# Softmax denominators turned and compacted on VectorE before the check and the reciprocal, with the steps of a two-layer graph kernel in a new order

## The chip, the cores and the metric

The kernel runs on one core of one Trainium2 chip. The metric is the device time of one launch in microseconds (us); lower is better. Engine names as in the profile: PE is TensorE (PEld its weight loads), DVE is VectorE, ACT is ScalarE, POOL is GpSimd, SP is SyncE, which issues the DMAs.

## The reference

128 graphs of 128 nodes with 256 features (float32) and an integer adjacency pass through two layers. Layer 0 is masked multi-head attention with a feed-forward block; layer 1 is two graph-attention (GAT) steps with a feed-forward block.

```python
# layer 0 (8 heads of 32, four relations; the random adjacency holds only 0 and 1)
q, k = src @ Wq + bq, src @ Wk + bk
attn = softmax(q k^T / sqrt(32), axis=-1)
out  = sum over r of (attn * (adj == r)) @ (src @ Wv[r] + bv[r])
x    = LN(src + out @ Wo + bo)
x    = LN(x + gelu(x @ W1 + b1) @ W2 + b2)
# layer 1
h = gat(gat(x, adj, W1, a1), adj, W2, a2)     # leaky_relu scores, softmax over axis 1
h = LN(x + h)
x = LN(h + relu(h @ w_ff1 + b_ff1) @ w_ff2 + b_ff2)
```

## The kernel before

`fast_pass` assumes that adj is 0 or 1 and that no softmax leaves a safe range without its maximum subtracted. It records extremes on the way (`c_adj`, `c_gat`, `c_att`), and the step `checks` compares them at the end. Only if one fails does `general_pass` compute everything again. In the profiled execution `fast_pass` alone does the work.

The 128 graphs go in 32 groups of 4 (`G`), so a group is 512 tokens. A group passes through steps written as Python generators: each `yield` ends one piece of a step, and a string of tokens says which piece of which step of which group comes next. `FRONT` covers the start, `STEADY` is used once for each middle group (29 times), `TAIL` ends. In a token `f:1*2`, `f` is the step, 1 the group relative to the current one, 2 the number of pieces. The steps: `q` projections, `a` attention, `n0`..`n3` layer norms, `t0`..`t2` the transposed copies of x, `f` the first feed-forward block, `l` the GAT layer, `k` the second feed-forward block, `in`, `rest` and `out` the loads and stores. The recording is under `manual_schedule`, so each engine executes its instructions in exactly the recorded order, and so does SP with its DMA issues. An engine that waits in its order holds all that stands behind it.

The feed-forward blocks and projections use Strassen-like products (7 in place of 8) into the PSUM banks `fa`, `fe` and `seeded`; DVE and ACT combine the parts. `seeded` is drained by ACT (`p16`) or DVE before PE adds the next product to it. A matmul instruction of float32 shows as two matmuls in the trace.

Attention does two graphs at a time, as "pair 0" and "pair 1". For one pair: `scores` (PE, tile `ps`), exp (ACT, tile `e`), `masked` (DVE, `pm` = e times adj), then `sums`. In `sums` the PE writes the unnormalised output into `pav`, and the denominators into `pden`, by a matmul with a block of ones of 32 columns. So each denominator, of one head and one query, stands 32 times below each other: rows 0 to 31 of `pden` are one head, and all 32 are equal. `pden` holds 128 x 512 numbers, of which 128 x 16 differ. ACT copies it into `rd` with a running sum for the check (L810) and runs over it a second time for the lower bound (L813); DVE takes the reciprocal of all 128 x 512 numbers, in two halves (L817, L819), and multiplies `pav` by it into `oT` (L822). `pden` of pair 0 lies in the bank `fe`, that of pair 1 in one of the two banks `s`; `pav` has one bank, `av`, for both pairs. From `oT` comes the output projection (`pwo`).

Of the kernel before, what the change touches and what calls it, by code (L numbers as in the profile page):

```python
# [99 lines left out]


FRONT = """
bo:0 q:0*4 a:0*3 q:0*2 a:0*5 q:0*2 a:0*3 output_bias q:1 a:0*2 n0:0 q:1*2 n0:0*2 q:1 a:1*2 n0:0*2
b1 a:1 q:1 w1 q:1 t0:0*3 bo:1 a:1 in:2 q:1 f:0*2 a:1*2 f:0*2 a:1*2 gelu a:1 q:1 f:0*3 wqk f:0 a:1
f:0 w2 f:0*4 gw f:0 a:1*2 gw f:0*3 gw f:0 a:1*2 f:0 n0:1 q:2 n0:1*4 f:0*2 q:2 f:0 gw q:2 t0:1*2
n1:0 q:2*2 t0:1 q:2 f:1 n1:0*3 u2 n1:0 q:2*2 f:1*3 q:2 t1:0*2 c1 q:2 f:1*3 l:0 f:1*2 u1 q:2 l:0*3
q:2 l:0*2 f:1 q:2*2 l:0 f:1 q:2 f:1 l:0 f:1 wv l:0 f:1 l:0*2 exp f:1 a:2 l:0*3 f:1 q:2 a:2 q:2*2
l:0 q:2 f:1*2 q:2*2 n2:0 q:2 n2:0 q:2 a:2 n2:0 f:1 q:2 n2:0 q:2 f:1 q:2*2 n2:0 f:1 q:2*2 t2:0*2
in:3 a:2*2 f:1 t2:0 n1:1 k:0 a:2 k:0*2 a:2 n1:1*4 a:2 k:0*3 t1:1*2 k:0 a:2 k:0*2 a:2 k:0 l:1 a:2
bo:2 k:0*3 l:1 k:0*2 a:2 k:0 l:1 a:2 k:0*2 a:2 l:1 n0:2 k:0 n0:2*3 q:3 l:1 k:0*2 n0:2  # L110
"""
STEADY = """
l:0 t0:1 q:2 t0:1*2 q:2 f:1 q:2*2 f:1 q:2 l:0 k:-1 f:1 q:2*2 f:1*2 n3:-1 f:1 l:0 gelu q:2*2 f:1
l:0 n3:-1 f:1 l:0 n3:-1 q:2*3 f:1*5 q:2*2 f:1 l:0*2 f:1 l:0 out:-1 f:1 a:2 l:0 rest:2 f:1 q:2
a:2*2 q:2*3 l:0 q:2*2 n2:0 q:2*2 n2:0*3 f:1*2 q:2*2 n2:0 f:1 q:2*2 f:1 exp t2:0 in:3 q:2*2 t2:0
f:1 n1:1 a:2*2 t2:0 k:0*3 a:2 n1:1 k:0 a:2 n1:1*3 a:2 k:0*2 a:2 k:0*3 t1:1 a:2 k:0 bo:2 t1:1 a:2
l:1 k:0*2 a:2 l:1 k:0 l:1 a:2*2 n0:2 k:0 n0:2 k:0 l:1 n0:2 k:0 n0:2 k:0 l:1 k:0*4 q:3 n0:2
"""
TAIL = """
k:-1 t0:1*3 f:1 l:0 f:1*2 l:0 f:1*3 n3:-1 l:0 gelu f:1*3 l:0 f:1 n3:-1*2 l:0*2 f:1*3 l:0*2 f:1  # L120
exp l:0 f:1*2 l:0 n2:0 f:1*2 n2:0*4 t2:0 f:1 out:-1 t2:0 f:1*3 n1:1 t2:0 k:0 n1:1 k:0*2 n1:1 k:0
n1:1*2 k:0*2 t1:1 k:0 t1:1 l:1 k:0 l:1*4 k:0 l:1 k:0*2 l:1 k:0*2 l:1*4 k:0 l:1*2 k:0 l:1 k:0 l:1
n2:1 k:0 n2:1*4 k:0*3 t2:1*2 k:0*2 t2:1 k:1*3 n3:0*2 k:1*4 n3:0 k:1 out:0 k:1*7 checks k:1*5
z:1*2 k:1*2 z:1
"""


# [8 lines left out]
def fast_pass(ctx, tc, a, out):  # L136
# [5 lines left out]
    nc = tc.nc  # L142
# [268 lines left out]

    def turned(S, i):
        n = f"{i}_{S['g']}"
        yT = w2p.tile([P, NCH, T], F32, tag="yT", name="yT_" + n)
        for p in range(G // 2):
            pT = S["pT", i, p].rearrange("p (h b c) t -> p h b c t", h=2, b=2)
            for c in range(NCH):
                o = yT[:, c, p * D : (p + 1) * D].bitcast(U16)
                nc.scalar.copy(  # L419
                    o.rearrange("p (b t h) -> p h b t", b=2, h=2), pT[:, :, :, c, :]  # L420
                )
            if p == 0:
                yield
        S["xT", i + 1] = yT
        yield
        if i == 1:
            return

        S["yS", i + 1] = ys = w1p.tile([P, 4, TH], F32, tag="yS", name="yS_" + n)
        a11, a21, a12, a22 = (yT[:, c, h * TH : (h + 1) * TH] for c in range(2) for h in range(2))  # L430
        nc.vector.tensor_sub(ys[:, 2], a11, a21)
        nc.vector.tensor_add(ys[:, 0], a21, a22)
        nc.vector.tensor_sub(ys[:, 1], a22, ys[:, 2])
        nc.vector.tensor_sub(ys[:, 3], a12, ys[:, 1])
        yield

    def ffn(S, i, wa, ba, func, wb_):

        n = f"{i}_{S['g']}"
        yT, ys, x = S["xT", i], S["yS", i], S["x"]  # L440
        a11, _, a12, a22 = (yT[:, c, h * TH : (h + 1) * TH] for c in range(2) for h in range(2))
        s1, s2, s3, s4 = (ys[:, m] for m in range(4))
        hT = w1p.tile([P, NF, T], F32, tag="hT", name="hT_" + n)
        h2 = w1p.tile([P, NF // 2, TH], F32, tag="h2", name="h2_" + n)
        h3 = w1p.tile([P, NF // 2, TH], F32, tag="h3", name="h3_" + n)
# [45 lines left out]
        pa = begun(0)  # L491
        nc.scalar.copy(seeded, pa)
        yield
        for r in range(RN):
            rs = slice(2 * r, 2 * r + 2)
            pe = ps_1.tile([P, T], F32, tag="fe", name=f"ph7_{n}_{r}")
            product(pe, T3, s3, r, True)
            p7 = w1p.tile([P, T], F32, tag="p7", name=f"p7_{n}_{r}")
            nc.scalar.copy(p7, pe)
            yield  # L500
            product(seeded, T2, s2, r)
            p16 = w1p.tile([P, T], F32, tag="p16", name=f"p16_{n}_{r}")
            nc.scalar.copy(p16, seeded)  # L503
            yield
            product(pa, B21, a12, r)
            activated(pa, r, 0, 0)
            yield
            product(seeded, T1, s1, r)
            nc.vector.tensor_add(hidden(1, 1, r), halves(seeded), halves(p7))  # L509
            activated(None, r, 1, 1)  # L510
            yield
            product(pe, T4, a22, r)
            nc.vector.tensor_add(hidden(0, 1, r), halves(pe), halves(p16))  # L513
            activated(None, r, 0, 1)
            yield
            if r + 1 < RN:
                pa = begun(r + 1)
                yield
            product(seeded, B22, s4, r)
            activated(seeded, r, 1, 0)  # L520

            nc.vector.tensor_sub(h3[:, rs], hidden(0, 0, r), hidden(0, 1, r))
            nc.vector.tensor_add(hidden(0, 1, r), hidden(0, 1, r), hidden(1, 1, r))
            nc.vector.tensor_sub(h2[:, rs], hidden(1, 1, r), h3[:, rs])
            if r + 1 < RN:
                nc.scalar.copy(seeded, pa)
            yield
# [245 lines left out]
    def sums(S, p):  # L773


        assert {(1, 0, p), (1, 1, p)} <= S["have"]
        e, pm = S["e", p], S["pm", p]
        n = f"{S['g']}_{p}"

        pool, tag = (ps_1, "fe") if p == 0 else (ps_s, "s")  # L780
        pden = pool.tile([P, 2, NCH, P], F32, tag=tag, name="pden_" + n)
        pav = ps_1.tile([P, 2, NCH, P], F32, tag="av", name="pav_" + n)

        def plain():
            for s in range(HC):
                nc.tensor.matmul(
                    pden[s * DH : (s + 1) * DH], k.ones, e[:, s], start=True, stop=True
                )


        late = S["g"] > 1
        if not late:
            plain()
        for u in range(2):
            v = S["v"][:, 2 * p + u]
            for c in range(NCH):
                for r, m in enumerate((e, pm)):
                    for s in range(HC):
                        d0 = r * D + c * P + s * DH
                        nc.tensor.matmul(  # L800
                            pav[s * DH : (s + 1) * DH, u, c, :],
                            v[:, d0 : d0 + DH], m[:, s, u, c, :],
                            start=(r == 0), stop=(r == 1),
                        )
# [5 lines left out]
        nc.scalar.activation(  # L810
            rd, pden, AF.Identity, accum_out=c_att[:, 1, g, p : p + 1]
        )
        nc.scalar.activation(  # L813
            pden, pden, AF.Relu, bias=k.lo, scale=-1.0, accum_out=c_att[:, 0, g, p : p + 1]
        )
        yield
        nc.vector.reciprocal(rd[:, 0], rd[:, 0])  # L817
        yield
        nc.vector.reciprocal(rd[:, 1], rd[:, 1])  # L819
        for u in range(2):  # L820
            bs = slice((2 * p + u) * P, (2 * p + u + 1) * P)
            nc.vector.tensor_mul(oT[:, :, bs], pav[:, u], rd[:, u])  # L822
        yield
# [139 lines left out]
    def checks():  # L963

        gat = c_gat.rearrange("p g l b -> p (g l b)")
        for i, (t, op) in enumerate(
            (
                (gat, ALU.min), (gat, ALU.max), (c_att[:, 1].rearrange("p g u -> p (g u)"), ALU.max),
                (c_att[:, 0].rearrange("p g u -> p (g u)"), ALU.max), (c_adj, ALU.max),
            )  # L970
        ):
            nc.vector.tensor_reduce(ext[:, i : i + 1], t, AX.X, op)
        nc.vector.tensor_scalar(ok[:, 0:1], ext[:, 0:1], LO, None, op0=ALU.is_ge)
        nc.vector.tensor_scalar(ok[:, 1:3], ext[:, 1:3], HI, None, op0=ALU.is_le)
        nc.vector.tensor_scalar(ok[:, 3:5], ext[:, 3:5], 0.0, None, op0=ALU.is_le)

# [415 lines left out]
```

## Time and profile before

| | before |
|---|---|
| median of 3 runs | 2732.59 us (2731.11 to 2733.99) |
| profiled execution, device time | 2731.53 us |
| its span, first to last instruction | 2729.7 us |
| granted TensorE clock, mean | 0.994 |
| PE / DVE / ACT / POOL busy | 98% / 85% / 64% / 5% |
| reciprocals of the denominators on DVE (L817, L819) | 128 of about 1.74 us |
| passes over the denominators on ACT (L810, L813) | 128, 596 and 657 ns, each with a read of its sum of 0.2 us |

The profiled execution is 1.83 us longer than its span and 1.06 us shorter than the median. Busy shares are averages over the whole span. The marker ACT L581 (one element through gelu or exp, which loads that table) stands twice in a group, and every second one comes 82.7 us after the one before in the middle of the span: this is the time of one group. A matmul's end is modelled in the trace, and a matmul that follows another starts before that end, so the PE's pace is read from the distance of starts rather than from its durations.

### The profile page before, as it was taken

What the parts mean: (1) busy time and instruction counts of PE and PEld (TensorE: products, weight loads), DVE (VectorE), ACT (ScalarE), POOL (GpSimd) and SP (SyncE); (2) the same over time, 40 slices, a digit from 0 to 9 for tenths busy, and PEclk for the clock granted to TensorE, in tenths of its full rate; (3) what the DMA queues carried; (4) which work ended last, traced back from release to release, by engine and by line L of the source; (5) the groups of instructions that cost most, each with busy time, mean ns of one, the idle gap of its engine ahead of it and who ended that gap; (6) DMA issues with size and microseconds to landing.
All of it is one profiled execution on the core that took longest, in us unless ns stands there. A gap on an engine that the chain in (4) does not pass through costs nothing.

```text
span 2729.7 us, 53540 instructions
## 1 busy us (share of the span) xinstructions
PE 2664.3 (98%) x20917; PEld 2308.5 (85%) x20917; DVE 2322.0 (85%) x5612; ACT 1750.6 (64%) x3777; POOL 142.3 (5%) x137
## 2 busy tenths in 40 slices
PE   8999999999999999999999999999999999999997
PEld 5887888888888888888888888889888888888876
DVE  4878889888889888889888898888898888888876
ACT  3556676666676666666665766666766666666663
POOL 0000000000000000000000000000000000000000
PEclk8999999999999999999999999999999999999999
DMA  6012111212121221121222112121112111212210
GB/s 188 16 28 55 51 44 36 59 48 52 48 54 36 57 49 51 44 52 43 51 55 51 44 37 57 50 54 48 50 36 59 47 51 44 59 36 51 47 36 25
DMA packets 271899, 136.43 MB, mean 50 GB/s; under 512 B 210092, under 2 KB 250392, under 8 KB 271640
## 3 DMA queue, kind: packets, MB, share of 16 engines
q1 hardware_dynamic: 270536, 132.55, 20.6%
q8 instruction: 166, 2.72, 0.4%
q14 instruction: 93, 0.76, 0.1%
q10 hardware_dynamic: 1104, 0.40, 0.1%
HBM read 65.68 MB, written 16.90 MB: 30 GB/s over the span
## 4 chain that ended last, share of the span: by engine, by line
PE 53%; DVE 34%; ACT 8%; issue 3%; DMA 1%; SPq 1%; POOL 0%; ACTq 0%; DVEq 0%; POOLq 0%
PE ph L454 9%; PE seeded L454 9%; PE po L463 9%; DVE x L379 6%; PE seeded L463 6%; DVE pm L768 4%; PE pw L919 4%; PE pwo L835 4%; DVE st L350 3%; ACT hT L478 3%; PE pqqa L680 3%; PE pqqb L680 3%; PE pav L800 2%; PE py L932 2%; DVE rd L817 2%
## 5 line engine op out<-in xcount | busy, mean ns | idle before, releaser
L393 ACT COPY planes<-x 128x512 uint16<-128x512 uint16 x384 | 216.5, 629 | 216.6 <-DVE x L379 216.6
L419 ACT COPY yT<-pT 128x512 uint16<-128x512 uint16 x384 | 267.3, 769 | 94.1 <-DMA pT<-planes 93.2
L368 POOL TENSOR_TENSOR rs<-rs,mhalf 128x4 f32<-128x4 f32 x129 | 140.1, 1086 | 2535.9 <-DVE rs L367 2535.9
L454 PE MATMUL seeded<-yS,w_L_gnn_w_ff 128*128 128x256 f32 x768 | 210.2, 396 | 2.0 <-DVE hT L509 0.7
L509 DVE TENSOR_TENSOR hT<-seeded,p 128x512 f32<-128x512 f32 x128 | 88.1, 688 | 139.2 <-PE seeded L454 139.1
L454 PE MATMUL seeded<-yS,w_L_gnn_W 128*128 128x256 f32 x768 | 201.9, 385 | 0.3 <-ACT p L503 0.2
L454 PE MATMUL ph<-yT,w_L_gnn_W 128*128 128x256 f32 x768 | 197.7, 380 | 3.8 <-ACT yT L419 3.8
L350 DVE BATCH_NORM_STATS2 st<-x 128x6 f32<-128x256 f32 x512 | 192.2, 417 | 6.8
L454 PE MATMUL ph<-yT,w_L_gnn_w_ff 128*128 128x256 f32 x768 | 195.4, 383 | 0.8 <-ACT hT L478 0.8
L454 PEld LDWEIGHTS seeded<-yS,w_L_gnn_w_ff 128*128 128x128 f32 x768 | 135.3, 189 | 69.2 <-ACT yT L419 24.3
L463 PEld LDWEIGHTS po<-w_L_gnn_W,hT 128*128 128x128 f32 x1536 | 186.1, 192 | 4.7
L463 PE MATMUL po<-w_L_gnn_w_ff,hT 128*128 128x128 f32 x1536 | 187.1, 275 | 0.0
L463 PE MATMUL po<-w_L_gnn_W,hT 128*128 128x128 f32 x1536 | 187.0, 275 | 0.0
L463 PEld LDWEIGHTS po<-w_L_gnn_w_ff,hT 128*128 128x128 f32 x1536 | 181.7, 192 | 1.7
L454 PEld LDWEIGHTS seeded<-yS,w_L_gnn_W 128*128 128x128 f32 x768 | 142.1, 190 | 30.2 <-ACT p L503 9.2
L454 PEld LDWEIGHTS ph<-yT,w_L_gnn_W 128*128 128x128 f32 x768 | 146.2, 191 | 24.6 <-ACT yT L419 4.6
L454 PEld LDWEIGHTS ph<-yT,w_L_gnn_w_ff 128*128 128x128 f32 x768 | 141.0, 190 | 25.7 <-ACT hT L478 1.4
L768 DVE TENSOR_TENSOR pm<-e,adj 128x512 f32<-128x512 f32 x256 | 159.2, 683 | 0.2 <-ACT e L758 0.2
L478 ACT ACTIVATE hT<-hT,c_L_gnn_b_ff 128x256 f32<-128x256 f32 x256 | 113.1, 514 | 70.6 <-DVE hT L513 41.1
L800 PE MATMUL pav<-pm,v 128*32 128x128 f32 x2048 | 126.0, 275 | 25.1 <-DVE v L695 19.2
L758 ACT ACTIVATE e<-ps 128x512 f32<-128x512 f32 x256 | 135.4, 602 | 4.8 <-PE ps L750 4.8
L463 PE MATMUL seeded<-w_L_gnn_W,hT 128*128 128x128 f32 x1024 | 130.6, 279 | 1.0 <-DVE hT L561 1.0
(196 smaller groups left out, 6350.6 us busy)
## 6 DMA issues: line engine op xcount, KB each, us to landing
xT<-in_xT_dram SPq DMA_DIRECT2D x32, 512.0 KB, 3.9
x<-in_x_dram SPq DMA_DIRECT2D x32, 512.0 KB, 6.2
out_dram<-x SPq DMA_DIRECT2D x31, 512.0 KB, 3.1
spread<-hbm SPq DMA_DIRECT2D x59, 256.0 KB, 3.2
adj<-in_adjT_dram SPq DMA_DIRECT2D x32, 256.0 KB, 4.5
pT<-planes SPq DMA_TRANSPOSE x192, 3.1
w_L_gnn_W<-in_L_gnn_W_dram SPq DMA_DIRECT2D x8, 256.0 KB, 8.3
w_L_gnn_w_ff<-in_L_gnn_w_ff_dram SPq DMA_DIRECT2D x8, 256.0 KB, 5.0
```

The costliest lines, as they stand in the source:

```text
L350: nc.vector.bn_stats(st[:, b % 2, :], S["x"][:, b, :])
L368: nc.gpsimd.tensor_tensor(rs[:, bs], rs[:, bs], k.mhalf[:, bs], op=ALU.pow)
L379: nc.vector.scalar_tensor_tensor(x[:, b, :], x[:, b, :], mv[:, b, 0:1] if first else rs[:, b : b + 1], g if first else be, op0=ALU.subtrac ...
L393: nc.scalar.copy(planes[:, :, b], words)
L419: nc.scalar.copy(o.rearrange("p (b t h) -> p h b t", b=2, h=2), pT[:, :, :, c, :])
L454: nc.tensor.matmul(bank[:, s * TH : (s + 1) * TH], wa[:, form, 0, f * P : (f + 1) * P], m, start=start and s == 0, stop=True, skip_group_c ...
L463: nc.tensor.matmul(bank[:, s * P : (s + 1) * P], m[:, f, s * P : (s + 1) * P], wb_[:, form, f, :], start=start and s + f == 0, stop=True, ...
L478: nc.scalar.activation(o[:, s], o[:, s] if src is None else src[:, s * TH : (s + 1) * TH], func, bias=ba[:, f : f + 1],)
L680: nc.tensor.matmul(bank[:, s * TH : (s + 1) * TH], *ops, start=start and s == 0, stop=True, skip_group_check=True,)
L758: nc.scalar.activation(e[:, s], pss[s], AF.Exp, scale=SCALE)
L768: nc.vector.tensor_mul(pm[:, s], S["e", p][:, s], S["ad"][:, pair(p), None, :].to_broadcast([P, 2, NCH, P]),)
L800: nc.tensor.matmul(pav[s * DH : (s + 1) * DH, u, c, :], v[:, d0 : d0 + DH], m[:, s, u, c, :], start=(r == 0), stop=(r == 1),)
```

## The change

In `sums`, ACT's two passes are gone. DVE turns each 32 x 32 block of `pden` into `rd` (one instruction, 128 x 512); after the turn the distinct denominators stand in every 32nd column, 16 in a partition. DVE takes their minimum and their sum for the check, then the reciprocal of these 128 x 16, and a second turn, fed by a broadcast view of the 16 columns, spreads them over `rd` again. The bank of `pden` is now freed by DVE's first turn. `checks` compares a minimum with the lower bound where it compared a sum of excesses with 0. The pieces of `sums` are cut at other places: one `yield` ahead of the turn, one behind the second turn. In `turned` the tile is entered earlier, in `ffn` the yS views are taken later; neither adds an instruction. The three order strings are new throughout.

```diff
 STEADY = """
-l:0 t0:1 q:2 t0:1*2 q:2 f:1 q:2*2 f:1 q:2 l:0 k:-1 f:1 q:2*2 f:1*2 n3:-1 f:1 l:0 gelu q:2*2 f:1
-l:0 n3:-1 f:1 l:0 n3:-1 q:2*3 f:1*5 q:2*2 f:1 l:0*2 f:1 l:0 out:-1 f:1 a:2 l:0 rest:2 f:1 q:2
-a:2*2 q:2*3 l:0 q:2*2 n2:0 q:2*2 n2:0*3 f:1*2 q:2*2 n2:0 f:1 q:2*2 f:1 exp t2:0 in:3 q:2*2 t2:0
-f:1 n1:1 a:2*2 t2:0 k:0*3 a:2 n1:1 k:0 a:2 n1:1*3 a:2 k:0*2 a:2 k:0*3 t1:1 a:2 k:0 bo:2 t1:1 a:2
-l:1 k:0*2 a:2 l:1 k:0 l:1 a:2*2 n0:2 k:0 n0:2 k:0 l:1 n0:2 k:0 n0:2 k:0 l:1 k:0*4 q:3 n0:2
+f:0 a:1*2 k:-1 a:1 n1:0 t2:-1 a:1 in:2 n1:0 a:1 k:-1*2 a:1 k:-1 n1:0 k:-1*3 n1:0 a:1 n1:0 t1:0
+k:-1*2 a:1 bo:1 l:0 k:-1 a:1 k:-1 a:1 t1:0 k:-1*2 a:1 k:-1 l:0 k:-1 n0:1 l:0 k:-1 n0:1*4 k:-1 q:2
+k:-1 q:2 l:0 k:-1 t0:1 l:0 t0:1 q:2 k:-1*2 q:2 l:0 t0:1 f:1*4 l:0*2 q:2 k:-1 f:1 n3:-1 f:1*2 l:0
+f:1 q:2*2 l:0 f:1 n3:-1*2 f:1 q:2*2 gelu f:1*3 q:2*2 out:-1 f:1 q:2 l:0 q:2 l:0 q:2*2 l:0 f:1 a:2
+l:0 f:1 q:2 a:2 rest:2 q:2*2 a:2 q:2 l:0 n2:0 q:2 f:1 q:2*3 n2:0*2 f:1 q:2*2 n2:0 q:2 f:1 q:2*3
+n2:0 t2:0 exp f:1 t2:0 f:1
 """
...
     def sums(S, p):
...
         g, oT = S["g"], S["oT"]
+        yield
         rd = w1p.tile([P, 2, NCH, P], F32, tag="rd", name="rd_" + n)
-        nc.scalar.activation(
-            rd, pden, AF.Identity, accum_out=c_att[:, 1, g, p : p + 1]
-        )
-        nc.scalar.activation(
-            pden, pden, AF.Relu, bias=k.lo, scale=-1.0, accum_out=c_att[:, 0, g, p : p + 1]
-        )
-        yield
-        nc.vector.reciprocal(rd[:, 0], rd[:, 0])
-        yield
-        nc.vector.reciprocal(rd[:, 1], rd[:, 1])
+        flat_rd = rd.rearrange("p u c i -> p (u c i)")
+        nc.vector.transpose(flat_rd, pden.rearrange("p u c i -> p (u c i)"))
+        each = flat_rd[:, ::DH]
+        nc.vector.tensor_reduce(c_att[:, 0, g, p : p + 1], each, AX.X, ALU.min)
+        nc.vector.tensor_reduce(c_att[:, 1, g, p : p + 1], each, AX.X, ALU.add)
+        rc = small.tile([P, T // DH], F32, tag="rc", name="rc_" + n)
+        nc.vector.reciprocal(rc, each)
+        nc.vector.transpose(
+            flat_rd.rearrange("p (k r) -> p k r", r=DH), rc[:, :, None].to_broadcast([P, T // DH, DH])
+        )
+        yield
         for u in range(2):
...
     def checks():
...
-                (gat, ALU.min), (gat, ALU.max), (c_att[:, 1].rearrange("p g u -> p (g u)"), ALU.max),
-                (c_att[:, 0].rearrange("p g u -> p (g u)"), ALU.max), (c_adj, ALU.max),
+                (gat, ALU.min), (c_att[:, 0].rearrange("p g u -> p (g u)"), ALU.min),
+                (gat, ALU.max), (c_att[:, 1].rearrange("p g u -> p (g u)"), ALU.max), (c_adj, ALU.max),
```

More of the change, by code (lines that the diff above doesn't have):

```diff
@@ L102 @@
 FRONT = """
[L103 to L107, printed above, removed]
@@ L108 @@
-l:0 q:2 f:1*2 q:2*2 n2:0 q:2 n2:0 q:2 a:2 n2:0 f:1 q:2 n2:0 q:2 f:1 q:2*2 n2:0 f:1 q:2*2 t2:0*2
-in:3 a:2*2 f:1 t2:0 n1:1 k:0 a:2 k:0*2 a:2 n1:1*4 a:2 k:0*3 t1:1*2 k:0 a:2 k:0*2 a:2 k:0 l:1 a:2
-bo:2 k:0*3 l:1 k:0*2 a:2 k:0 l:1 a:2 k:0*2 a:2 l:1 n0:2 k:0 n0:2*3 q:3 l:1 k:0*2 n0:2
+q:0*6 a:0*3 q:0 a:0*2 b1 bo:0 a:0*2 q:1*2 a:0 q:0 q:1 gw q:1 w1 a:0 a:1 a:0 a:1 a:0*2 wqk a:1 a:0
+q:1*2 n0:0 q:1 n0:0*2 a:1 n0:0 a:1*2 n0:0 a:1*3 gelu t0:0 q:1 w2 a:1 t0:0*2 f:0 a:1 in:2
+output_bias f:0 a:1 f:0*2 bo:1 f:0*2 a:1 f:0 q:2 a:1 q:2 gw q:2 f:0*2 q:2 f:0 gw n0:1 f:0 q:2
@@ L111 @@
+f:0*2 n0:1 gw q:2 f:0*3 n0:1 f:0 n0:1 f:0*3 q:2 f:0*2 t0:1 n0:1 t0:1 n1:0 f:1 n1:0 t0:1 n1:0*2 c1
+f:1*2 n1:0 q:2 f:1 q:2 t1:0 f:1 q:2 f:1 t1:0 f:1 q:2*2 u2 l:0 f:1 l:0 f:1 q:2 l:0 wv l:0*2 f:1
+q:2 u1 q:2 a:2 l:0 a:2 f:1 l:0 f:1*2 l:0 f:1*2 l:0 q:2 l:0 a:2 q:2 l:0*4 q:2*2 f:1*2 q:2 l:0 exp
+q:2 n2:0 q:2*4 n2:0*3 f:1 q:2 n2:0 f:1 q:2*3 t2:0 f:1 t2:0 f:1
 """
 STEADY = """
-l:0 t0:1 q:2 t0:1*2 q:2 f:1 q:2*2 f:1 q:2 l:0 k:-1 f:1 q:2*2 f:1*2 n3:-1 f:1 l:0 gelu q:2*2 f:1
-l:0 n3:-1 f:1 l:0 n3:-1 q:2*3 f:1*5 q:2*2 f:1 l:0*2 f:1 l:0 out:-1 f:1 a:2 l:0 rest:2 f:1 q:2
@@ L118 @@
+f:1 q:2*2 l:0 f:1 n3:-1*2 f:1 q:2*2 gelu f:1*3 q:2*2 out:-1 f:1 q:2 l:0 q:2 l:0 q:2*2 l:0 f:1 a:2
+l:0 f:1 q:2 a:2 rest:2 q:2*2 a:2 q:2 l:0 n2:0 q:2 f:1 q:2*3 n2:0*2 f:1 q:2*2 n2:0 q:2 f:1 q:2*3
+n2:0 t2:0 exp f:1 t2:0 f:1
 """
 TAIL = """
-k:-1 t0:1*3 f:1 l:0 f:1*2 l:0 f:1*3 n3:-1 l:0 gelu f:1*3 l:0 f:1 n3:-1*2 l:0*2 f:1*3 l:0*2 f:1
-exp l:0 f:1*2 l:0 n2:0 f:1*2 n2:0*4 t2:0 f:1 out:-1 t2:0 f:1*3 n1:1 t2:0 k:0 n1:1 k:0*2 n1:1 k:0
-n1:1*2 k:0*2 t1:1 k:0 t1:1 l:1 k:0 l:1*4 k:0 l:1 k:0*2 l:1 k:0*2 l:1*4 k:0 l:1*2 k:0 l:1 k:0 l:1
@@ L123 @@
-n2:1 k:0 n2:1*4 k:0*3 t2:1*2 k:0*2 t2:1 k:1*3 n3:0*2 k:1*4 n3:0 k:1 out:0 k:1*7 checks k:1*5
-z:1*2 k:1*2 z:1
+f:0 a:1 n1:0 a:1 t2:-1 in:2 k:-1*2 a:1*2 k:-1 n1:0*2 k:-1 a:1*2 k:-1*2 a:1 n1:0*2 a:1 k:-1 t1:0
+k:-1 l:0 a:1 k:-1*2 bo:1 k:-1 a:1*2 t1:0 l:0*2 k:-1 n0:1 k:-1 n0:1 k:-1 n0:1 k:-1 l:0 n0:1 k:-1*2
+n0:1 l:0*2 t0:1 l:0 k:-1*3 l:0*2 t0:1 k:-1 l:0*2 t0:1 l:0 k:-1 f:1*2 l:0 f:1*2 gelu l:0 f:1*2 l:0
+f:1 n2:0 f:1 n3:-1 f:1*5 n2:0*2 f:1*4 n2:0*2 exp f:1 t2:0*2 f:1*4 n1:1 t2:0 n1:1 k:0*3 n1:1*2 k:0
@@ L125 @@
+n1:1 k:0*2 t1:1*2 k:0 q:2 l:1 k:0 l:1 n3:-1 l:1*4 k:0 l:1 k:0*2 l:1*3 n3:-1 l:1*3 k:0*2 l:1 k:0*2
+l:1 n2:1 k:0 n2:1 k:0 out:-1 n2:1*2 k:0 n2:1 k:0 t2:1 k:0 t2:1 k:0 t2:1 k:0 k:1*2 n3:0 k:1*12
+n3:0 k:1*3 n3:0 checks k:1 out:0 k:1*2 z:1*2 k:1*2 z:1
 """
@@ L413, in turned @@
         n = f"{i}_{S['g']}"
-        yT = w2p.tile([P, NCH, T], F32, tag="yT", name="yT_" + n)
+        S["xT", i + 1] = yT = w2p.tile([P, NCH, T], F32, tag="yT", name="yT_" + n)
         for p in range(G // 2):
@@ L423, in turned @@
                 yield
-        S["xT", i + 1] = yT
         yield
@@ L439, in ffn @@
         n = f"{i}_{S['g']}"
-        yT, ys, x = S["xT", i], S["yS", i], S["x"]
+        yT, x = S["xT", i], S["x"]
         a11, _, a12, a22 = (yT[:, c, h * TH : (h + 1) * TH] for c in range(2) for h in range(2))
-        s1, s2, s3, s4 = (ys[:, m] for m in range(4))
         hT = w1p.tile([P, NF, T], F32, tag="hT", name="hT_" + n)
@@ L493, in ffn @@
         yield
+        s1, s2, s3, s4 = (S["yS", i][:, m] for m in range(4))
         for r in range(RN):
@@ L972, in checks @@
             nc.vector.tensor_reduce(ext[:, i : i + 1], t, AX.X, op)
-        nc.vector.tensor_scalar(ok[:, 0:1], ext[:, 0:1], LO, None, op0=ALU.is_ge)
-        nc.vector.tensor_scalar(ok[:, 1:3], ext[:, 1:3], HI, None, op0=ALU.is_le)
-        nc.vector.tensor_scalar(ok[:, 3:5], ext[:, 3:5], 0.0, None, op0=ALU.is_le)
+        nc.vector.tensor_scalar(ok[:, 0:2], ext[:, 0:2], LO, None, op0=ALU.is_ge)
+        nc.vector.tensor_scalar(ok[:, 2:4], ext[:, 2:4], HI, None, op0=ALU.is_le)
+        nc.vector.tensor_scalar(ok[:, 4:5], ext[:, 4:5], 0.0, None, op0=ALU.is_le)
     ET = mybir.EngineType
```

## The prediction

> **What bounds the kernel now.** I read the page first (busy shares, chain), then two windows of one period, then chain and timeline inside the first.
>
> ```profile
> PE 2664.3 (98%) x20917; PEld 2308.5 (85%) x20917; DVE 2322.0 (85%) x5612; ACT 1750.6 (64%) x3777; POOL 142.3 (5%) x137
> ...
> PE 53%; DVE 34%; ACT 8%; issue 3%; DMA 1%; SPq 1%; POOL 0%; ACTq 0%; DVEq 0%; POOLq 0%
> ```
>
> PE looks full, yet a third of the chain runs through DVE. One period (82.71 us) in two windows; the columns are length, then PE, PEld, DVE, ACT and POOL busy:
>
> ```profile
> 1080.14:1103.30 23.16, 22.35 (x250) 16.89 (x249) 23.02 (x46) 18.02 (x40) 1.05 (x1) 1.00 0.32 67
> 1103.30:1162.85 59.55, 59.55 (x404) 54.52 (x403) 49.09 (x130) 36.56 (x80) 3.33 (x3) 1.00 0.18 42
> ```
>
> In the first 23 us, attention beside the end of `f` and the start of `k`, DVE is never free (23.02 of 23.16); behind it DVE has 10 us to spare. I call the first window the tight stage. The chain inside it (start, us, what) is one DVE queue from 1080.12 to 1097.92, with two reciprocals in it:
>
> ```profile
> 1080.12 1.20 DVE hT L561 x2
> ...
> 1084.17 0.60 DVE v L695
> ...
> 1088.88 1.66 DVE rd L817
> 1090.55 1.49 DVE x L379 x4
> 1092.04 1.66 DVE rd L819
> ...
> 1096.02 1.90 DVE pm L768 x3
> 1097.92 0.04 issue
> 1097.96 1.61 PE pav L800 x49
> ```
>
> What PE loses shows in the distance of starts (timeline):
>
> ```profile
> 1083.78 0.43 PE L800 MATMUL pav<-e,v 128*32 128x128 f32 x8
> 1084.82 0.42 PE L800 MATMUL pav<-pm,v 128*32 128x128 f32 x8 [0.61 <-DVE v L695]
> 1085.06 0.40 PE L800 MATMUL pav<-e,v 128*32 128x128 f32 x8
> ...
> 1107.64 3.62 PE L835 MATMUL pwo<-w_L_gnn_Wo,oT 128*128 128x256 f32 x16
> 1111.09 1.03 PE L454 MATMUL seeded<-yS,w_L_gnn_w_ff 128*128 128x256 f32 x4
> 1111.96 1.95 PE L463 MATMUL po<-w_L_gnn_w_ff,hT 128*128 128x128 f32 x16
> ```
>
> Eight `pav` matmuls undisturbed take 0.24 us here and 0.22 further on; the first eight take 1.04, since v is late. Sixteen of 256 columns take 3.45 us (1107.64 to 1111.09), so four take 0.86; sixteen of 128 take 1.79, eight `pw` 1.75, 64 `pav` 1.75, 32 score matmuls 1.10, eight `pden` 0.88.
>
> PE's own work in the tight stage, by these distances: three of `pvqb` 0.65, `seeded` L463 1.79, `pvqa` 0.86, `pav` twice 3.50, `pden` twice 1.76, scores 1.10, nine quadruples of L454 7.76, a last `seeded` 0.86, `pw` 1.75, the next begun 0.1: 20.1 us of 23.16. **PE loses 3.0 us a period here**; the same count over the whole period gives 79.4 of 82.71, so the rest loses 0.3.
>
> **The change, part by part.** The rows that price it (count, busy us and mean ns, idle before):
>
> ```profile
> L817 DVE RECIPROCAL rd<-rd 128x256 f32<-128x256 f32 x64 | 111.8, 1747 | 3.9 <-ACT rd L810 3.9
> L768 DVE TENSOR_TENSOR pm<-e,adj 128x512 f32<-128x512 f32 x256 | 159.2, 683 | 0.2 <-ACT e L758 0.2
> L907 DVE RECIPROCAL gr<-gr 128x4 f32<-128x4 f32 x64 | 11.4, 178 | 2.2
> L972 DVE TENSOR_REDUCE ext<-c_att 128x1 f32<-128x64 f32 x2 | 0.3, 208 | 0.0
> ```
>
> *Removed on DVE:* two reciprocals a pair. Each blocks the queue 1.66 us (chain), 3.32 a pair.
>
> *Added on DVE:* two turns, two reduces, one reciprocal of 16 columns. No trace shows a turn. The nearest row by size is L768, 683 ns for 128x512 (the next starts after 0.60); all other 128x512 rows of DVE lie at 658 to 694, PSUM sources among them, so I take 0.69. Lower end: 0.42, the row of 256 columns, if two went at a time; it would win little, since DVE would then no longer be what PE waits for. Upper ends: two passes, 1.37 less one start, 1.23, and the reciprocal's rate, 3.3 (rivals 2 and 1). A reduce by L972: 208 ns for 64 columns, 412 for 256, so 1.06 ns a column and about 160 ns for 16; behind each other they cost 0.08. A reciprocal: (1747 - 178)/252 = 6.2 ns a column, so 0.25 us for 16. An operation that needs the one before starts 0.035 behind its end, any other 0.08 before it. A pair costs 0.725 + 0.08 + 0.08 + 0.285 + 0.61 = 1.78 us: 1.54 less, 3.1 us a period. [...]
>
> *Removed on ACT:* 0.60 + 0.20 + 0.65 + 0.20, less overlaps of 0.1 each, so 1.4 us a pair. PE's waits on ACT's `seeded` and `p` copies in the tight stage (0.1 each, L492, L503) shrink with it.
>
> *Bank of `pden`:* freed by the first turn in place of ACT's second pass. Behind the turn's wait for PE stand the affines of `n1`, `oT` and `pm`; their turn comes after `pden` in any case.
>
> *The order.* Lay it on PE's pace, from the start of the last product of `f` (`seeded` B22). PE: 1.79, `pav` 1.75, `pden` 0.86, scores 1.10, seven quadruples of `k` 6.04, the `e` part of the next `pav` 0.22: it wants `pm` of pair 1 from 11.8. DVE from the same instant: x and its statistics 0.45 + 0.97, a wait for B22 until 2.0, x and statistics again 1.4, rs 0.1, yS 1.47, so the turn starts at 5.0 (`pden` ended at 4.6); 1.78 for the turns, half an affine 1.6, `oT` 0.66, `pm` 2.4: done at 11.5. PE is no longer late. In the old order 3.32 of reciprocals, the other half affine (1.6) and `hT` L509, L513 (1.2) stood ahead of `pm`; the last two now stand behind it. Next: `hT` 1.2, affine 1.6, h 1.9, so the second turn runs from 16.1 to 16.8, and frees the bank that PE's second `pw` wants at 16.9. **This is the narrowest place: 0.1 us.** The old tight spot before the first `pav` goes too: v is ready at 0.4, wanted at 2.0.
>
> *Moved DMAs.* `in` now stands beside the first scores of pair 1, its xT is used some 35 us later and lands in 3.9; adj is issued 10 us ahead of `pm` and lands in 4.5; x has 39 us for 6.2. The three pairs of transposes keep SP 1.23 us each and land in 3.1; the pair for `pw` is next late if ACT's planes slip, and holds nothing behind it on SP that is due. POOL only does the rs powers (1.05 us), each covered by a half affine.
>
> *FRONT and TAIL* idle PE for 9.9 us before 77.1, 8.7 to 224.8, and 20.4 after 2637: 39 us, mostly fills of chains that any order has. Bounds: half of it more, half less. I take 5 less.
>
> **Sum.** Of 3.0 us a period I keep 0.5 for about five places where a wait that ends just in time costs 0.1 us, as now at four matmuls of 256 columns in the tight stage (0.97 from 1094.96 to 1095.93 in place of 0.86). 30 stages (groups 2 to 31) x 2.5 = 75, plus 5: 80. Profiled execution 2731.5 - 80 = 2651.5; the median lies 1.1 higher: **2652 us**, own range 2630 to 2675.
>
> **Rivals.**
> 1. *The turns are slow, and DVE stays the bound (slower).* Place: the DVE queue between `pden` and `pm`, and before `pw`. Each turn that takes e us more costs 4e a period, less about 0.9 of slack in the two places. The gain (2.5 + 5/30 = 2.7) is gone at e = 0.9, a turn of 1.6 us. At 2.0 us: 4 x 1.31 - 0.9 - 2.7 = +1.6 a period, 2732.6 + 48 = 2781. For: one DVE row, the reciprocal, does run at 6 ns a column. Against: every other 128x512 row runs at 683 to 694. Chance 0.08.
> 2. *The turns take two passes, 1.23 us:* 4 x 0.54 - 0.9 = 1.3 a period, half the gain: 2691. Chance 0.09.
> 3. *The order makes new waits of its own:* `pw` behind the second turn, `seeded` behind ACT's `p16` while ACT does four exp (2.4 us), `pw` behind yT and its transposes. At 0.5 us each, 1.5 a period: 2731.5 - 30 x 1.0 - 5 + 1, about 2698. Chance 0.13.
> 4. *PE is full already.* Taken by its busy time PE idles only 2234.90 - 2212.41 = 22.5 us from 224.8 to 2459.7, and no order can win more: 2732.6 - 23 = 2710, or nothing (2733) if the idle time is not DVE's. Against it: 1.04 us for eight `pav` that take 0.22. [...] Chance 0.05, 0.03 of it for no difference.
>
> **How the numbers follow.** Forecast 0.65; rivals as above. The range reaches from all of the waits gone (30 x 3.3 + 8, so 2626) to past rivals 2 and 3: 2625 to 2705. A difference of 0.2% (5.5 us) is about what can be told from none. Faster 0.87: forecast, 2, 3, and 0.02 of rival 4, less 0.02 for worse cases of 3; same 0.03; slower 0.10, rival 1 and those.
>
> **What would show it.** Right: a period of 80.0 to 80.5 us; turns near 0.7 us; no `pav` wait on v or `pm`; DVE no longer full in the stage. Wrong: turns above 1.2 us; PE waiting at `pw` for `rd`; a period above 81.5.

## The result: 3.0% faster, 2649.6 us

| | before | after |
|---|---|---|
| median | 2732.15 us (2731.11 to 2733.99) | 2649.62 us (2648.62 to 2651.39) |
| span of the profiled execution | 2729.7 us | 2646.8 us |
| one group in the steady part | 82.71 us | 80.58 us |

The ratio is 0.9698, 95% interval 0.9681 to 0.9715. The page of the changed kernel, busy times and the chain by engine:

```profile
PE 2617.9 (99%) x20917; PEld 2308.3 (87%) x20917; DVE 2229.0 (84%) x5804; ACT 1672.5 (63%) x3519; POOL 133.3 (5%) x137
...
PE 95%; DVE 2%; ACT 1%; DMA 1%; issue 0%; POOL 0%; POOLq 0%; ACTq 0%; DVEq 0%
```

DVE's part of the chain fell from 34% to 2% and ACT's from 8% to 1%, although DVE is still busy 84% of the span: an engine that is nearly as busy as before has left the path. One period in two windows; the first reaches from the last product of `f` (`seeded` B22) through the first eight `pw`, the tight stage of the prediction in the new order (columns: length, then PE, PEld, DVE, ACT, POOL busy, then granted clock, DMA share, GB/s):

```profile
1120.31:1138.92 18.61, 18.61 (x239) 14.77 (x238) 18.02 (x47) 14.34 (x29) 1.05 (x1) 1.00 0.28 64
1138.92:1200.89 61.97, 61.97 (x416) 56.92 (x414) 51.27 (x136) 38.99 (x84) 3.02 (x3) 1.00 0.20 46
```

DVE has only 0.6 us free in the stage, and yet no matmul waits for it any more. The two are seen side by side in the timelines of that stage. First DVE (start, length):

```profile
1120.01 0.68 DVE L696 TENSOR_TENSOR v<-pvqa,bv 128x512 f32<-128x512 f32 x1
...
1125.31 0.71 DVE L813 STREAM_TRANSPOSE rd<-pden 128x512 f32<-128x512 f32 x1
1126.05 0.18 DVE L815 TENSOR_REDUCE c_att<-rd 128x1 f32<-128x16 f32 x1
...
1129.36 2.48 DVE L769 TENSOR_TENSOR pm<-e,adj 128x512 f32<-128x512 f32 x4
...
1136.47 0.71 DVE L813 STREAM_TRANSPOSE rd<-pden 128x512 f32<-128x512 f32 x1
```

Then PE in the same stretch:

```profile
1120.31 1.95 PE L463 MATMUL seeded<-w_L_gnn_W,hT 128*128 128x128 f32 x16
1122.19 0.42 PE L801 MATMUL pav<-e,v 128*32 128x128 f32 x8
1122.44 0.40 PE L801 MATMUL pav<-pm,v 128*32 128x128 f32 x8
...
1132.83 0.40 PE L801 MATMUL pav<-pm,v 128*32 128x128 f32 x8
...
1136.30 1.03 PE L454 MATMUL ph<-yS,w_L_gnn_w_ff 128*128 128x256 f32 x4
1137.16 1.92 PE L922 MATMUL pw<-wu,yT 128*128 128x260 f32 x8
```

v is done at 1120.69, 1.5 us before the first `pav`. `pm` of pair 1 is done at 1131.84, 1.0 us before PE takes it at 1132.83. Pair 1's first turn ends at 1137.18 and frees the bank that the second `pw` takes at 1138.03. None of these starts carries a wait.

The new instructions (count, busy us and mean ns):

```profile
L813 DVE STREAM_TRANSPOSE rd<-pden 128x512 f32<-128x512 f32 x64 | 45.3, 708 | 0.6 <-PE pden L787 0.6
L819 DVE STREAM_TRANSPOSE rd<-rc 128x512 f32<-128x512 f32 x64 | 45.5, 711 | 2.2
L815 DVE TENSOR_REDUCE c_att<-rd 128x1 f32<-128x16 f32 x64 | 11.5, 179 | 2.2
L818 DVE RECIPROCAL rc<-rd 128x16 f32<-128x16 f32 x64 | 15.6, 244 | 0.0
```

A turn takes 0.71 us, from PSUM and from a broadcast view alike.

### The profile page after: what moved, and what is told of

It is laid out like the page before. It is cut to its first block, busy times and chain, and to the rows that moved or that the text cites. A ratio compares the mean times of both kernels' runs of the same rounds, so it can differ in the third digit from the quotient of the medians.

```text
span 2646.8 us, 53404 instructions
## 1 busy us (share of the span) xinstructions
PE 2617.9 (99%) x20917; PEld 2308.3 (87%) x20917; DVE 2229.0 (84%) x5804; ACT 1672.5 (63%) x3519; POOL 133.3 (5%) x137
## 4 chain that ended last, share of the span: by engine, by line
PE 95%; DVE 2%; ACT 1%; DMA 1%; issue 0%; POOL 0%; POOLq 0%; ACTq 0%; DVEq 0%
PE po L463 17%; PE ph L454 16%; PE seeded L454 13%; PE seeded L463 12%; PE pw L922 4%; PE pav L801 4%; PE pwo L838 4%; PE pvqa L681 4%; PE pqqa L681 4%; PE pvqb L681 3%; PE pqqb L681 3%; PE ps L751 3%; PE py L935 2%; PE pg L948 2%; PE pden L787 2%; DMA pT<-planes 1%
## 5 line engine op out<-in xcount | busy, mean ns | idle before, releaser
L370 POOL TENSOR_TENSOR rs<-rs,mhalf 128x4 f32<-128x4 f32 x129 | 131.2, 1017 | 2459.9 <-DVE rs L369 2413.3
L454 PE MATMUL ph<-yT,w_L_gnn_W 128*128 128x256 f32 x768 | 192.4, 379 | 0.0
L478 ACT ACTIVATE hT<-hT,c_L_gnn_b_ff 128x256 f32<-128x256 f32 x256 | 109.2, 497 | 83.8 <-DVE hT L510 83.8
L478 ACT ACTIVATE hT<-hT,c_L_gnn_b 128x256 f32<-128x256 f32 x256 | 109.1, 497 | 31.4 <-DVE hT L510 29.6
L922 PE MATMUL pw<-wu,yT 128*128 128x260 f32 x512 | 124.6, 385 | 2.5 <-ACT yT L421 2.1
```

Of the source, the lines that this page charges most:

```text
L370: nc.gpsimd.tensor_tensor(rs[:, bs], rs[:, bs], k.mhalf[:, bs], op=ALU.pow)
L454: nc.tensor.matmul(bank[:, s * TH : (s + 1) * TH], wa[:, form, 0, f * P : (f + 1) * P], m, start=start and s == 0, stop=True, skip_group_c ...
L478: nc.scalar.activation(o[:, s], o[:, s] if src is None else src[:, s * TH : (s + 1) * TH], func, bias=ba[:, f : f + 1],)
L922: nc.tensor.matmul(pw[:, :NU], yT[:, c, b * P : (b + 1) * P], wu[:, c, :], start=(c == 0), stop=(c == NCH - 1),)
```

## The experiments

Times below are medians; each ratio stands against runs of the kernel before on the same chip. "Period" is the time of one group in the steady part, by the distance of the first `pav` matmuls of two groups, or of the ACT marker where matmuls were added. Beside that marker the trace of before has a table load (1.28 us) at only 2 of 62 places; most stand ahead of the gelu at L478 (33) and the exp at L897 (31). It marks the period all the same. Three stretches of a span are compared as well: the front (start to the first `pav` of group 2), the middle (from there to that of group 31) and the tail.

### Each half of the change alone

Order alone keeps the new order strings and takes the old denominators back; turns alone does the reverse:

```diff
# order alone, against the changed kernel
-        nc.vector.transpose(flat_rd, pden...)      # and the reduces, the short reciprocal, the second turn
+        nc.scalar.activation(rd, pden, AF.Identity, accum_out=c_att[:, 1, g, p : p + 1])
+        nc.scalar.activation(pden, pden, AF.Relu, bias=k.lo, scale=-1.0, accum_out=c_att[:, 0, g, p : p + 1])
+        yield
+        nc.vector.reciprocal(rd[:, 0], rd[:, 0])
+        yield
+        nc.vector.reciprocal(rd[:, 1], rd[:, 1])
# turns alone, against the changed kernel
-FRONT, STEADY, TAIL = the new strings
+FRONT, STEADY, TAIL = the strings of before
```

> The new order with the old denominators: ACT's two passes behind the pden matmuls, two reciprocals of 256 columns a pair. Theory (both parts are needed, the turns most in front of pm): the new order has pm of pair 1 ready 0.3 us before PE wants it and holds 1.8 us of turned denominators ahead of it; with 3.3 us of reciprocals there pm is 1.2 to 1.5 us late in each period, so the period is 80.6 + 1.3 = 81.9 us and the time about 2650 + 30 x 1.3 = 2689 us (2675 to 2705). Rival A (the order is what brings it, the turns are not needed): 2650 to 2657 us. Rival B (the order is worth nothing without the turns): 2725 us or more, PE waiting 2.5 us or more a period at pav or pw.

> The turned denominators in the old order (they stand where the first reciprocal stood). Theory: VectorE has 23.0 us of work in the 23.2 us of the tight stage of before, of which the turns take 3.1 us away, and PE itself needs 20.1; so most of the 3.0 us that PE loses there goes, less what late starts in the old order keep (0.5 to 1.0): a period of 80.5 to 81.2 us instead of 82.7, 2660 to 2690 us, 2675 the likeliest. Rival A (the order does it): 2715 us or more. Rival B (the order adds nothing): 2650 us, the period 80.6.

| | time, us | ratio (95%) | period | front | middle | tail |
|---|---|---|---|---|---|---|
| before | 2731.75 | | 82.71 | 165.6 | 2407.9 | 156.2 |
| turns alone | 2727.90 | 0.9989 (0.9979 to 0.9998) | 82.64 | 166.3 | 2406.0 | 155.5 |
| order alone | 2731.96 | 1.0003 (0.9993 to 1.0013) | 83.22 | 158.0 | 2414.4 | 157.5 |
| both | 2649.62 | 0.9698 (0.9681 to 0.9715) | 80.58 | 154.0 | 2339.8 | 153.1 |

(The row of both is the result above, against a before of 2732.15.) Both expectations were wrong by over 40 us. The order alone is worth nothing, the turns alone 4 us (the interval nearly touches 1), and the two together 82. Rival B of the order run named this; rival A of the turns run has the time (2715 us or more), but its reason, that the order alone brings the gain, is refuted.

The nothing of the order alone is a sum of two that happen to cancel: it wins 7.6 us in the front and 6.9 in the first interval behind it (90.33 to 83.39), and loses 13.4 in the 28 others and 1.3 in the tail. In the steady part it is a loss.

**Where the turns alone lose it again.** PE's waits in that trace (engine, line, what it waited for: total us, times, longest), first PE, then its weight loads:

```profile
PE pav L799 <- DVE v L694: 19.1, 30, 1.4
...
PEld pw L920 <- DVE rd L811: 16.9, 29, 0.6
PEld ph L452 <- DVE rd L811: 11.8, 30, 0.7
PEld pav L799 <- DVE pm L767: 8.6, 29, 0.3
```

By the distance of starts, `pav` and `pden` of pair 1 take 3.17 us a period instead of 3.58, since `pm` comes earlier: 0.41 won. But the banks of `pden` are now freed by DVE. The first `ph` behind the scores needs pair 0's bank and takes 1.12 us instead of 0.97; the first eight `pw` need pair 1's and take 2.19 instead of 1.75: 0.59 lost. Two quadruples (four matmuls of L452, 256 columns each) take 0.11 less each; the net is about 0.05 us a period won, 0.07 by the periods. The 0.8 us at v stay: in the old order v's last product stands directly ahead of `pav`, and no denominator stands between them.

**Where the order alone loses it.** A typical period of that trace, on PE and then on ACT:

```profile
1005.80 1.03 PE L454 MATMUL ph<-yS,w_L_gnn_w_ff 128*128 128x256 f32 x4
1008.04 2.21 PE L920 MATMUL pw<-wu,yT 128*128 128x260 f32 x8 [1.21 <-ACT yT L421]
```

```profile
1004.94 0.60 ACT L811 ACTIVATE rd<-pden 128x512 f32<-128x512 f32 x1 [0.33 <-PE pden L787]
...
1005.52 0.65 ACT L814 ACTIVATE pden<-pden,lo 128x512 f32<-128x512 f32 x1
...
1006.19 1.13 ACT L395 COPY planes<-x 128x512 uint16<-128x512 uint16 x2
1007.22 1.39 ACT L421 COPY yT<-pT 128x512 uint16<-128x512 uint16 x2
```

ACT's two passes over `pden` stand ahead of the `planes` and `yT` copies, and PE waits for yT: from `ph` to `pw` it is 2.24 us instead of 0.86. Pair 1's `pav` and `pden` take 3.57 instead of 2.74 (`pm` late behind the reciprocals), the first eight `pw` 2.04 instead of 1.75, and the quadruples of the stage 0.15 more: 1.38 + 0.83 + 0.29 + 0.15 = 2.65, against 83.22 - 80.58 = 2.64 measured. My expectation had only the 0.83 and some: it had DVE in view and not ACT.

### The order alone, with ACT's passes moved

Only pair 1's passes are moved, one step later in the order string and so behind the `planes` copies:

```diff
         g, oT = S["g"], S["oT"]
+        if p:
+            yield
         rd = w1p.tile(...)
...
-        yield
+        if not p:
+            yield
         nc.vector.reciprocal(rd[:, 0], rd[:, 0])
```

> The order-alone kernel with pair 1's two ScalarE passes over pden one step later, behind the copies into planes (pair 0 is as it was; both reciprocals of pair 1 follow the passes). In the order-alone trace the passes stand ahead of the planes copies, which so come 1.35 us later, the transposes land later, and PE waits 1.36 us for yT ahead of the first pw. Theory: this wait goes, pm's 0.6 us and what the longer reciprocals cost at pwo stay: a period of 81.9 us, 2692 us (2685 to 2705). Rival (VectorE's 3.1 us more are the bound of the period, wherever ScalarE's passes stand): 2720 us or more.

Measured: 2789.05 us, ratio 1.0217 (1.0200 to 1.0234), the period changing between 84.35 and about 86.0 us. The theory fell, in an instructive way. What PE waited for in its first `pw`, then one such wait, and ACT ahead of it:

```profile
PE pw L923 <- ACT pden L816: 68.1, 29, 2.4
...
1200.68 1.15 PE L923 MATMUL pw<-wu,yT 128*128 128x260 f32 x4 [2.35 <-ACT pden L816]
...
1195.14 1.14 ACT L395 COPY planes<-x 128x512 uint16<-128x512 uint16 x2
1196.18 1.39 ACT L421 COPY yT<-pT 128x512 uint16<-128x512 uint16 x2
...
1199.25 0.62 ACT L813 ACTIVATE rd<-pden 128x512 f32<-128x512 f32 x1
...
1199.83 0.67 ACT L816 ACTIVATE pden<-pden,lo 128x512 f32<-128x512 f32 x1
```

The wait for yT is gone (3.1 us in the whole run); a longer one for the bank of `pden`, freed by the second pass, stands in its place: the first eight `pw` take 4.55 us. One step later in the string is far later on ACT: the yT copies and three more pieces stand ahead of the passes too, and they start 2.97 us behind the `planes` copies. Of the two places tried for ACT's passes in the new order, ahead of the copies they make yT late, this far behind they keep the bank. The turn takes the passes off ACT, and frees the bank by one instruction of 0.71 us on DVE. In these two places the order pays only with the turns. A place directly behind the yT copies was not tried; by this trace `pw` would wait there for about 0.9 us (an estimate: passes from 1197.44, `pw` 1.43 behind their start as here, wanted at 1197.97). The 0.83 us at `pm`, which the reciprocals cost, would stay.

Part of this run's time is not a wait at all. PE stands still for the same time in every group (2.73 us from the fourth `pw` matmul to the fifth), but in 17 of the 29 steady groups the granted clock is down to 0.50 behind it (0.985 in the mean of this run, 0.994 to 0.995 in the kernel before on the same chip). Two stretches behind such a wait (columns as in the result, so the clock is third from the end):

```profile
1115.00:1117.00 2.00, 2.00 (x5) 1.61 (x6) 2.00 (x4) 0.07 (x2) 0.00 (x0) 0.50 0.04 8
1201.00:1203.00 2.00, 2.00 (x11) 1.76 (x10) 2.00 (x4) 0.60 (x2) 0.00 (x0) 1.00 0.00 0
```

In the first the second four `pw` take 1.89 us and the quadruple behind them 1.43, in the other 0.98 and 0.86. These groups are the ones of about 86 us: some 28 us of the run are the clock's. Why the clock falls in some groups and not in others the runs do not show.

### What is left to gain on VectorE: the first turn alone

```diff
         nc.vector.transpose(flat_rd, pden.rearrange("p u c i -> p (u c i)"))
-        each = flat_rd[:, ::DH]                    # and both reduces, the reciprocal, the second turn;
                                                   # c_att is filled with 1.0 once instead
```

> The changed kernel without the two reduces, the reciprocal and the second turn; the product takes the first turn's plane. Left out: the division (a multiplication by denominators in a wrong arrangement stands in its place) and the check of the denominators. VectorE saves 1.1 us a pair, 2.2 us a period. Theory (after the change PE is not kept waiting by VectorE; the 1.1 to 1.2 us a period above PE's pace are lost at PE itself, where its matmuls change tile shape): within 6 us of the changed kernel, 2644 to 2652 us. Rival (these 1.15 us are still VectorE's, at the bank of the second pw and at pm): 15 to 35 us faster, 2615 to 2635 us.

> The old order with the first turn alone: no reduces, no reciprocal, no second turn. Left out: the division (a multiplication by denominators in a wrong arrangement stands in its place) and the check of the denominators. VectorE has 2.2 us a period less than in the turns-alone kernel. Theory (in the old order PE no longer waits for the denominators' time on VectorE once they are turned; what is left is v, finished directly ahead of the first pav, 0.8 us, ScalarE's chain to hT, some 0.6, and the shape changes; only the 0.44 us at the second pw goes): a period of 82.2 us, 2714 us (2708 to 2722). Rival (VectorE's time is still the bound in the old order): up to 2.2 us a period gone, 2660 to 2690 us.

New order: 2650.71 us, ratio 0.9706 (0.9690 to 0.9722), period 80.57 against 80.58: nothing. After the change PE waits for no microsecond of the 2.2 that these instructions take. Old order: 2729.56 us, ratio 0.9996 (0.9986 to 1.0006), period 82.64: nothing either, where I had expected 0.44 a period at `pw`. That was a slip: the bank is freed by the first turn, which was left in its place. The run shows that in the old order, too, DVE's work as such was not the bound once the denominators were turned; with the same work the new order takes 80.58 us.

### The old order with single steps moved

```diff
# bo behind pair 1's turns
-... k:0*3 t1:1 a:2 k:0 bo:2 t1:1 a:2
+... k:0*3 t1:1 a:2 k:0 t1:1 a:2 bo:2
# and, in the second kernel, v's last products ahead of the last product of f
-... f:1*2 q:2*2 n2:0 f:1 q:2*2 f:1 exp t2:0 in:3 q:2*2 t2:0
+... f:1 q:2*2 f:1 n2:0 f:1 q:2*4 f:1 exp t2:0 in:3 t2:0
```

> The turns-alone kernel with one step moved: bo (x plus bias and the statistics of adj, 1.8 us on VectorE) stands behind pair 1's turns instead of ahead of them. Theory: the second turn then ends 1.2 us earlier, ahead of the moment PE wants its bank for the second pw, and the 0.44 us that the turns-alone trace shows there go: a period of 82.2 us, 2715 us (2710 to 2720). Rival (the wait only moves to ScalarE's chain behind it): no change, 2725 to 2730 us.

> The kernel with bo behind the turns, and the last two products and sums of v moved ahead of the last product of f, so that PE has 1.9 us of other work between the last v product and the first pav. Theory: of the 0.8 us that PE waits at the first pav and the 0.27 at the two products ahead of it 0.8 to 1.0 go: a period of 81.3 us, 2688 us (2680 to 2700). With it two local moves bring about half of what the whole new order brings. Rival (VectorE's queue ahead of v is what is late, not its place behind the product): within 6 us of the kernel with bo behind alone.

`bo` behind: 2716.38 us, ratio 0.9951 (0.9935 to 0.9968), period 82.20; the 0.44 us at `pw` are gone, as expected. With v moved too: 2720.79 us, ratio 0.9966 (0.9955 to 0.9977), the rival and a little worse. Its waits:

```profile
PE pav L799 <- DVE v L694: 14.9, 30, 1.4
PE ph L452 <- DVE rd L811: 14.6, 30, 1.6
```

v's product now ends 1.9 us ahead of `pav`, but DVE reaches it hardly sooner: the first eight `pav` take 0.88 us instead of 1.04. What was won there and at the `pvqa` ahead of it came back at the first `ph`, 1.58 us instead of 1.12, behind pair 0's turn. So of the single moves tried in the old order one recovers about 11 us more than the turns alone, and the next one nothing; the wait that is left is again for DVE's queue, in another place.

### How slow could a turn be

Each turn is done twice, or three times, with the same result:

```diff
-        nc.vector.transpose(flat_rd, pden...)      # likewise the second turn
+        nc.vector.transpose(flat_rd, pden...)
+        nc.vector.transpose(flat_rd, pden...)
```

> The changed kernel with every turn done twice (the same turn again, same result): each costs one more start, 0.61 to 0.63 us, four times a period. By the rule of the prediction (4e less 0.9 of slack, e = 0.61) the period grows by 1.5 us and the time by 46 us, to 2696 us (2680 to 2705). Rival (VectorE has room: in the 26.5 us around the attention of group 12 it is busy for 24.1, so 2.4 us are idle and four more turns of 0.61 just fit): 2650 to 2660 us, less than 0.3 us a period.

> The changed kernel with every turn done three times. Theory (the rule of the prediction, and 82.18 against 80.58 us with each turn twice): 4 x 1.26 - 0.9 = 4.1 us a period more, 84.7 us, 2650 + 30 x 4.1 = 2773 us (2765 to 2782). It bears on the point from which slow turns would have made the change a loss. Rival (the next 0.63 us cost only as much as the first): 80.58 + 3.2 = 83.8 us, 2746 us.

Twice: 2698.77 us, ratio 0.9885 (0.9868 to 0.9901), period 82.18. Thrice: 2769.80 us, ratio 1.0149 (1.0132 to 1.0165), period 84.46. Both fall into the ranges, though the reckoning behind them was off twice. A repeated turn writes what the one before wrote and starts 0.745 us behind it, not 0.63:

```profile
1148.37 0.71 DVE L813 STREAM_TRANSPOSE rd<-pden 128x512 f32<-128x512 f32 x1
1149.11 0.72 DVE L814 STREAM_TRANSPOSE rd<-pden 128x512 f32<-128x512 f32 x1
1149.86 0.18 DVE L816 TENSOR_REDUCE c_att<-rd 128x1 f32<-128x16 f32 x1
```

With e = 0.745 and 1.49 the periods grew by 1.60 and 3.88: 3e less 0.6, not 4e less 0.9. The slope fits three turns that count: both of pair 0, ahead of `pm`, and the first of pair 1, which frees the bank. The second of pair 1 stands ahead of nothing that is due. With each turn twice the places are those that the prediction named; with three a further one is added, the first `ph` behind pair 0's bank (third line, from that run):

```profile
PE pw L926 <- DVE rd L814: 18.1, 29, 0.6
PE pav L801 <- DVE pm L769: 5.5, 32, 0.2
...
PE ph L454 <- DVE rd L815: 15.6, 30, 1.2
```

With each turn twice the first eight `pw` take 2.79 us instead of 1.75.

### What PE itself still loses

One matmul of 128 columns over the whole array is added to every block of `pav`, ahead of it or in its middle; later matmuls overwrite its result:

```diff
         for u in range(2):
             v = S["v"][:, 2 * p + u]
+            if u == 0:      # ahead of the block; u == 1: inside it
+                nc.tensor.matmul(pav[:, u, 0, :], k.ident, k.ident, start=True, stop=True)
```

> The changed kernel with one more matmul of 128 columns over the whole array (its result is overwritten) directly ahead of each block of pav, behind other matmuls over the whole array. Its own distance is 0.11 us (the pr matmul), so two a period make 0.22 us: 30 x 0.22 = 7, 2656 us (2652 to 2659).

> The same matmul in the middle of each block of pav, between its two halves, so that PE goes from tiles of 32 columns to the whole array and back once more. Theory (each change of tile shape costs about 0.1 us, which is what most of the 1.15 us a period above PE's pace are): 4 changes a period more, 0.4 us, so 12 us above the kernel with the matmul ahead of the block, 2668 us (2662 to 2673). Rival (the 0.1 us pieces are late semaphores of other engines): equal to that kernel within 3 us.

Ahead: 2662.62 us, ratio 0.9754 (0.9738 to 0.9770), period 81.02. Inside: 2684.62 us, ratio 0.9836 (0.9819 to 0.9852), period 81.69. Inside a block, on PE:

```profile
1138.12 0.40 PE L803 MATMUL pav<-e,v 128*32 128x128 f32 x8
1138.34 0.40 PE L803 MATMUL pav<-pm,v 128*32 128x128 f32 x8
1138.67 0.49 PE L798 MATMUL pav<-ident 128*128 128x128 f32 x2
1139.09 0.43 PE L803 MATMUL pav<-e,v 128*32 128x128 f32 x8
```

Eight `pav` take 0.33 us instead of 0.22 ahead of the added matmul, which takes 0.42. Ahead of a block it costs 0.22 a time (81.02 - 80.58, by two): it is two matmuls in the trace, and I had counted one. The difference of the two kernels, 81.69 - 81.02 = 0.67 us a period, is four changes between tiles of 128 x 128 and of 128 x 32: 0.17 us each, more than the 0.1 expected. The rival (no difference) falls. So the runs show that a change costs, and its size; what PE does in that time they do not show.

## Why the prediction was right

**The layout of the stage** held nearly to the tenth. From the start of the last product of `f` at 1120.31, in us:

| | forecast | measured |
|---|---|---|
| v ready / first `pav` | 0.4 / 2.0 | 0.4 / 1.9 |
| pair 0's first turn starts | 5.0 | 5.0 |
| `pm` of pair 1 done / wanted | 11.5 / 11.8 | 11.5 / 12.5 |
| pair 1's first turn | 16.1 to 16.8 | 16.2 to 16.9 |
| bank wanted by the second `pw` | 16.9 | 17.7 |

DVE's column is right. PE's is 0.7 to 0.8 too early from pair 1's `pm` on, and so the "narrowest place" of 0.1 us has 0.85. The turn (0.71 for 0.69), the reduces (0.18 and 0.17 for 0.16) and the reciprocal (0.24 for 0.25) were priced well.

Of its own signs, turns near 0.7 us and no `pav` wait on v or `pm` came out. The period, 80.58, lies just past the 80.0 to 80.5 that it gave, and DVE is still 97% busy in the stage (18.02 of 18.61 us), so "no longer full" holds by very little.

**Mis-sized: what PE keeps losing.** The same count as for before gives 17.66 us of PE's own work between 1120.31 and 1138.92 (1.79 for `seeded`, 3.50 `pav`, 1.76 `pden`, 1.10 scores, 7.76 for nine quadruples, 1.75 `pw`), so 0.95 of 18.61 is lost there, where 0.5 was kept. Over the period it is 80.58 - 79.4 = 1.2 instead of 0.8. I put the 0.1 us pieces down to waits that end just in time. About 0.6 of the stage's 0.95 stands in six pieces at five changes of tile shape: `seeded` 1.88 for 1.79, `pden` 0.97 for 0.88, the quadruple behind the scores 0.97 for 0.86, eight `ph` 1.82 for 1.73, then `pden` 0.97 and `seeded` 0.97 again. They were there before and stay. That the change of shape is the cause in each of them was not tried. Most of the rest, 0.33, stands in three quadruples around the `seeded` that PE starts at 1129.80, 0.05 us behind the end of ACT's copy `p` (L504); the prediction had expected such waits to shrink, and three quadruples there lost 0.25 before. Thirty stages at 2.13 are 64 us, not 75.

**Mis-sized the other way: the two ends.** The span fell by 82.9 us: 11.6 in the front, 9.6 in the first interval behind it (90.33 to 80.75), 58.5 in the 28 others and 3.1 in the tail. With 64 for the stages some 19 fall to start and end, where I took 5 of at most 20. The 11 us too many and the 14 too few nearly cancel: the total of 2652 is better than its terms. So the time is hit so closely by luck; the mechanism does not hang on it. Of the front's 11.6, 7.6 come with the order alone (165.6 to 158.0), and 6.9 of the first interval's 9.6; the prediction's bound of 20 held, its choice of 5 did not.

**Incomplete: what the gain hangs on.** The sum priced DVE's queue and took ACT's relief (1.4 us a pair) as a small help. The order-alone runs show that it counts as much as the reciprocals: with ACT's passes in the two places tried in the new order, PE waits 1.38 us more a period at yT, or longer for the bank. And the loss of 3.0 us a period before was not the reciprocals' alone: without them, in the old order, all of it but 0.07 stayed. The prediction's layout of old and new order held this without saying so; the sentence on 3.1 us saved a period invites the wrong reading.

**The rivals.** Slow turns (1): the place was right, the price was 3e - 0.6; between the times with twice and thrice, taken as a line, the loss reaches the gain of 82.5 at e = 1.09, a turn of 1.8 us and not 1.6. Two passes (2) did not occur. New waits of the order (3): they occurred in both single halves, not in the whole; the `pw` behind a turn is real in the old order (0.44 us). PE full already (4): 82 us were won with 22.5 us of visible idle time. For the same 20917 matmuls PE's busy time fell from 2664.3 to 2617.9 us, so before it held more than the work; the weight loads' stayed (2308.5 and 2308.3 us, 85% and 87% of the span).

## What to carry to other kernels

When a hand-laid order and a cheaper operation come together, lay every engine's queue on the pace of the engine that must not wait, for the new order as a whole; the value of either part alone need not say anything about the sum (here 0 and 4 us against 82). Ask of each new instruction which bank it frees and who waits for it, not only how long it takes. A queue that is 99% busy in a window (DVE here, 23.02 of 23.16 us; the turns alone took work from it and won 4 us) need not be all that the others wait for: take work out of it, and if nothing moves, look at its order and at the banks that it frees.

## What the runs showed of the hardware beyond that

- DVE turns 128 x 512 float32 in 0.71 us, from PSUM (708 ns) or from a broadcast view of 16 columns (711 ns) alike. A second turn into the same tile starts 0.745 us behind the first (1148.37 to 1149.11 above), another DVE instruction 0.63 behind a turn (1126.51 to 1127.14).
- A change of PE between whole-array tiles and tiles of 32 columns costs about 0.17 us inside a block of `pav` (four a period cost 0.67). The pieces at the five changes of a tight stage are 0.6 us longer together. Whether an order with fewer changes would win them was not tried.
- After a standstill of PE that is the same in every group (2.73 us between two `pw` starts), the granted clock was 0.50 in 17 of 29 groups, and stayed at 1.00 in the others. The eight matmuls shown behind the standstill then took 3.32 us (1.89 + 1.43) instead of 1.84 (0.98 + 0.86).
